# A four-stage transformer kernel on one core: routing rows turned by VectorE, norms' biases on GpSimd, and two more early products

## The chip, the cores and the metric

The kernel runs on one core of one Trainium2 chip. A core has five engines, each with its own instruction queue: TensorE (PE in the profile; its weight loads are shown apart as PEld), VectorE (DVE), ScalarE (ACT), GpSimd (POOL) and SyncE (SP), which issues most transfers. The engines wait for each other through semaphores; each takes its own instructions in order. SBUF and PSUM are memories of 128 partitions; TensorE writes its results to PSUM, from where DVE and ACT fetch them.

The metric is the time of one execution on the device, in microseconds (us). The kernel before took 1895.78 us, the median of 3 runs (1893.15 to 1896.54).

## The reference, cut to what matters

Sixteen sequences of 256 rows x 256 features go through four gated sublayers, all in 32-bit floats:

```
x = x + tanh(g_xattn[0]) * perceiver_attention(ctx, norm(x))     # stage 0: 16 heads of 64
x = x + tanh(g_ffn[0])   * experts(norm(x))                      # stage 1: 8 experts, 2 for each row
x = x + tanh(g_xattn[1]) * attention(norm(x), ctx, ctx)          # stage 2: 16 heads of 16
x = x + tanh(g_ffn[1])   * gated_linear_attention(norm(x))       # stage 3
```

`norm` is (x - mean) / sqrt(variance + 1e-5) over a row's 256 features. In stage 0 the row is normalised once by the outer norm (`y`) and once more by the attention's own (`xn`); the 77 context rows of each sequence are normalised too (`cn`). The experts' part needs the router first: `softmax(norm(x) @ router_w.T)` over 8 experts, the two largest of each row, their weights, and for each chosen expert `row @ expert_weights[e]`. The product with the router contracts over the features, so it needs the normalised rows with features on the partitions, that is turned.

## The kernel before, in words

The work is cut by sequence ("block" b, 0 to 15). A block's rows are two tiles of 128 rows, so a tile `x[b]` is 128 partitions x 2 x 256. Stage 0 takes about 960 us, and the routing of stage 1 is woven into it: while block b is in attention, block b-1 is normalised, turned and multiplied with the router, and block b-2 is ranked and scattered to the experts' lists in memory.

Stage 0 (`stage0_fast`, from line 548) runs over units (b, g), four units g = 0 to 3 a block, each with four heads. In a unit the engines get, in this order:

- `ahead_of[g]` (line 740): small work of the routing and statistics of later blocks. For g = 2: `route.weigh` of b-2 and `route.stats` of b-1.
- `scores` (line 671): products of queries and keys into three PSUM pairs `sc`, each followed by an exponential on ACT into `e`. The first pair reads the first half of `qk`, the second pair also the second half, from its second quarter on.
- `behind_scores[g]` (line 742): for g = 2 `route.norm` of b-1, which makes the normalised rows `rxn` on ACT.
- `sums` (line 689): POOL adds up `es` and `esum`.
- `values` (line 698) of the unit before: products into `o`, then on DVE a reciprocal and a product into `oT`.
- for g = 1 the turn of the next block's attention input and the projection of the block before.
- `behind_values[g]` (line 746): for g = 2 `route.ranks` of b-2 and `route.turn` of b-1, for g = 3 `route.logits` of b-1, which reads the turned rows `rxnT`.
- for g = 2 `all_values` of the next block (line 630): 16 records of products `v` (24 where a new tile of context rows comes in), with the halves copied from PSUM by ACT and then DVE.
- `heads` (line 657), twice: queries and keys of the next unit. PE writes a pair, ACT copies the queries and then DVE the keys into `qk`, which the next unit's `scores` reads.

All these calls go through `dve`, `act`, `pool` and `pe`, wrappers (`Pinned`, line 42) that keep the instructions of each engine in the order in which they are written. The order by hand is thus the order of each queue. PSUM has four pairs in stage 0, handed out in turn: a new pair waits for the readers of the pair four places before it.

`Route.turn` (line 404) turns the two row tiles of `rxn` with four PE transposes (128x128) into one PSUM pair `rtr`, from which ACT copies 128 x 512 elements to `rxnT`. It is called for blocks 0 to 14 in stage 0, and for block 15 at the start of stage 1 (line 1176).

The norms are in three steps. `moments` (line 199) has DVE compute mean and variance (`bst`, `mv`), and then a scale `rs[:, 0]` = (variance + eps)^-0.5, by POOL in two instructions or, with `by_act`, by ACT. `normed` (line 215) has DVE compute the bias `rs[:, 1]` = -mean x scale, and then ACT apply scale and bias to the 256 features of each row tile. `moments` is called for `x`, `y` and the context in stage 0 and for the routing, in stage 2's preparation (`Prepare.stats`, line 1230) and in stage 3 (`stats`, line 1631). Stage 3 has a `norm` of its own, which reads mean and scale but no bias.

Before the first unit (lines 759 to 769) the norms of block 0 go one after the other, with `warm` products in between: products of 256 columns on PE whose results nobody reads. Each fp32 product of this kind is two records in the profile.

Only `layers` with checks on (the fast version) is described here; a second copy behind a test at the end runs only if bounds are broken.

Of the kernel before, what the change touches and what calls it, by code (L numbers as in the profile page):

```python
# [10 lines left out]
F32 = mybir.dt.float32  # L11
I32 = mybir.dt.int32
AF = mybir.ActivationFunctionType
ALU = mybir.AluOpType
# [3 lines left out]
P = 128  # L18
B, S, D = 16, 256, 256
# [54 lines left out]
def layers(ctx: ExitStack, tc: tile.TileContext, t, out, check):  # L74
# [7 lines left out]
    def const(name, shape, dtype=F32):  # L82
        return cp.tile(list(shape), dtype, tag=name, name=name)
# [22 lines left out]
    ws1 = s1.enter_context(tc.tile_pool(name="s1w", bufs=1, side="right"))  # L106
# [7 lines left out]
    def c_count(j):  # L114
        return min(P, c_rows - P * j)

    def c_pieces(b):

        lo, hi = b * S2, (b + 1) * S2
        return [(j, max(lo, P * j) - P * j, max(lo, P * j) - lo, min(hi, P * j + P) - max(lo, P * j))  # L120
                for j in range(lo // P, (hi - 1) // P + 1)]

    def load_c(b):
        if b in c_new:
            j, n = c_new[b], c_count(c_new[b])
            cs[b] = ctxs.tile([P, D], F32, tag="c", name="c")
            nc.sync.dma_start(out=cs[b][:n], in_=t["ctx"].rearrange("b s d -> (b s) d")[P * j:P * j + n])
# [36 lines left out]
    ident = const("ident", [P, P])  # L164
# [10 lines left out]
    dve, act, pool, pe = (Pinned(tc, x) for x in (nc.vector, nc.scalar, nc.gpsimd, nc.tensor))  # L175
# [23 lines left out]
    def moments(src, p=P, n=2, by_act=False):  # L199
        mv = st.tile([P, 2, 2], F32, tag="mv", name="mv")  # L200
        rs = st.tile([P, 2, 2], F32, tag="rs", name="rs")
        bst = st.tile([P, 2, 6], F32, tag="bst", name="bst")
        for i in range(n):
            dve.bn_stats(bst[:p, i, :], src[:, i, :])
        for i in range(n):
            dve.bn_aggr(mv[:p, i, :], bst[:p, i, :])
        if by_act:
            act.activation(rs[:p, 0, :n], mv[:p, :n, 1], AF.Ln, bias=eps[:p])
            act.activation(rs[:p, 0, :n], rs[:p, 0, :n], AF.Exp, scale=-0.5)
            return mv, rs  # L210
        pool.tensor_scalar(rs[:p, 0, :n], mv[:p, :n, 1], 1.0, EPS, ALU.mult, ALU.add)
        pool.tensor_tensor(rs[:p, 0, :n], rs[:p, 0, :n], nhalf[:p, :n], ALU.pow)
        return mv, rs

    def normed(dst, src, mv, rs, p=P, n=2):
        dve.scalar_tensor_tensor(rs[:p, 1, :n], mv[:p, :n, 0], -1.0, rs[:p, 0, :n], ALU.mult, ALU.mult)
        for i in range(n):
            act.activation(dst[:, i, :], src[:, i, :], AF.Identity, bias=rs[:p, 1, i:i + 1],
                           scale=rs[:p, 0, i:i + 1])
# [165 lines left out]
    class Route:  # L385
# [11 lines left out]
        def stats(self, b):  # L397
            self.mv[b] = moments(xs[b])
# [3 lines left out]
            normed(self.xn[b], xs[b], *self.mv.pop(b))  # L402

        def turn(self, b, bank):
            self.xnT[b] = ws1.tile([P, 2, S], F32, tag="rxnT", name="rxnT")
            ps = bank("rtr")
            for k in range(2):
                for i in range(2):
                    pe.transpose(ps[:, (2 * k + i) * P:(2 * k + i + 1) * P], self.xn[b][:, i, k * P:(k + 1) * P], ident)
            act.copy(self.xnT[b], ps.rearrange("p (k s) -> p k s", k=2))  # L410

        def logits(self, b, bank):
            ps, xnT = bank("rt"), self.xnT.pop(b)
# [117 lines left out]
    if fast:  # L531
        route = Route()
# [15 lines left out]
    def stage0_fast():  # L548
        with ExitStack() as sx:
# [8 lines left out]
            def bank(name):  # L558
                return pair(name)[:, 0, :]
# [3 lines left out]
            xn, cn, kvT, v, oT, ctxT = {}, {}, {}, {}, {}, {}  # L563
# [5 lines left out]
            y, mvs, tallies = {}, {}, []  # L569

            def norm_c(b):
                if b in c_new:
                    n = c_count(c_new[b])
                    mvs[b, "c"] = moments(cs[b][:n].unsqueeze(1), n, 1)

            def norm_x(b):
                mvs[b, "x"] = moments(xs[b])

            def norm_y(b):
                mvs[b, "y"] = moments(y[b])  # L580

            def normed_y(b):
                y[b] = w1.tile([P, 2, D], F32, tag="y", name="y")
                normed(y[b], xs[b], *mvs.pop((b, "x")))
# [32 lines left out]
            def some_values(x, n):  # L617

                both = pair("v")
                for h in range(2):  # L620
                    for k in range(2):
                        pe.matmul(both[:n, h, :], x[:, k, :], wkv0[:, k, 1024 + h * 512:1024 + (h + 1) * 512],
                                         start=k == 0, stop=k == 1)
                return both

            def copied(to, both, n):
                act.copy(to[:n, :512], both[:n, 0, :])
                dve.tensor_copy(to[:n, 512:], both[:n, 1, :])

            def all_values(b, *between):  # L630

                v[b] = w2.tile([P, 3, 1024], F32, tag="v", name="v")
                between = list(between)
                if b in c_new:
                    j = c_new[b]
                    n = c_count(j)
                    both = some_values(ctxT[j][:, :, :n], n)
                    vc = w1.tile([P, 1024], F32, tag="vc", name="vc")
                    copied(vc, both, n)
                    if b == 0:  # L640
                        copied(v[b][:, 2, :], both, S2)
                    for to in range(1, B):
                        for jj, at, row, n in c_pieces(to):
                            if jj == j:
                                nc.sync.dma_start(out=vctx[to][row:row + n], in_=vc[at:at + n, :])
                if b > 0:
                    nc.sync.dma_start(out=v[b][:S2, 2, :], in_=vctx[b])
                for c in range(2):
                    copied(v[b][:, c, :], some_values(kvT[b][:, :, chunks[c]], P), P)
                    if between:  # L650
                        between.pop(0)()
                for x in between:
                    x()
# [72 lines left out]
            def tally():  # L726
                for rd, to in tallies:
                    act.activation(rd, rd, AF.Identity, accum_out=to)
                tallies.clear()

            def project(b):
                both = pair("proj")
                for i in range(2):
                    for m in range(8):
# [8 lines left out]
                             1: [(route.scatter, -3, 2)],  # L743
                             2: [(route.norm, -1), (route.scatter, -3, 3)],
                             3: [(normed_y, 2), (route.scatter, -2, 0)]}
            behind_values = {2: [(route.ranks, -2, bank), (route.turn, -1, bank)], 3: [(route.logits, -1, bank)]}

            def run(steps, b, g):
                for f, d, *a in steps.get(g, ()):
                    if 0 <= b + d < B:  # L750
                        f(b + d, *a)

            def warm(src, n):

                ps = bank("warm")
                for _ in range(n):
                    pe.matmul(ps[:, :D], ones, src, start=True, stop=True)
# [2 lines left out]
            warm(xs[0][:, 0, :], 3)  # L760
            normed_y(0)
            mvs[0, "y"] = moments(y[0], by_act=True)
            warm(y[0][:, 1, :], 2)
            norm_c(0)
            normed_all(0)
            turn(0)
# [5 lines left out]
            for n, (b, g) in enumerate(units):  # L772
                ahead = units[n + 1] if n + 1 < len(units) else None
                if n > 0:
                    run(ahead_of, b, g)
                now = scores(b, g)
                if g == 0 and b + 2 < B:
                    load_c(b + 2)
                if n == 0:

                    norm_c(1)
                    norm_x(1)
                    normed_y(1)
                    norm_y(1)
                else:
                    run(behind_scores, b, g)
                if n == 1:
                    normed_all(1)
                    clear_rows()
                now = sums(*now)  # L790
                if behind is not None:
                    values(*behind, by_chunk=n == 1)
                if g == 1 and b + 1 < B:
                    turn(b + 1)
                if g == 1 and b > 0:
                    project(b - 1)
                run(behind_values, b, g)
                if g == 2 and b + 1 < B:
                    all_values(b + 1, *route.weighted(b - 2))
                if ahead is not None:  # L800
                    heads(*ahead, 0)
                    heads(*ahead, 1)
                if g == 2 and b + 1 == B:
                    pieces = route.weighted(b - 2)
                    pieces[0]()
                if g == 3 and b + 1 == B:
                    pieces[1]()
                    pieces[2]()
                tally()
                behind = now  # L810
# [1339 lines left out]
```

## Time and profile before

| | |
|---|---|
| median of 3 runs | 1895.78 us |
| the profiled execution | 1900.88 us |
| its span, first to last instruction | 1899.1 us |
| mean granted TensorE clock | 0.993 |
| PE busy | 1872.1 us, 99% |
| PEld busy | 1310.1 us, 69% |
| DVE busy | 1085.0 us, 57% |
| ACT busy | 867.4 us, 46% |
| POOL busy | 986.0 us, 52% |
| stage 0 | about 11 to 960 us |
| stage 1, experts | about 960 to 1045 us alone, then with stage 2's start |
| stage 2 | to about 1220 us |
| stage 3 | to the end |

How to read it: busy time is the time in which an engine has at least one instruction running, as a share of the span. Products on PE are pipelined, so that PE at 99% isn't PE at its peak. The chain of work that ended last is followed back from the last instruction, at each step to what released it; an engine that has most of the chain is the bound. In timeline rows come start, length, engine, line, instruction, the written and the read tile, shapes, a count, and in brackets the idle time of the engine before it with what ended it. Tiles go by their names in the program with numbers left out: `rtr` is the pair of the routing's turns, `rxn` and `rxnT` are the routing's normalised rows and the turned ones, `rs` the scales and biases, `rd` the reciprocals. The line L50 is the wrapper's own line, which nearly all instructions share.

### The profile page before, as it was taken

Reading aid. Unit: us, or ns where it says so; the run is one execution under the profiler, and the core shown is the slowest. Engines: PE = TensorE matmul, PEld = TensorE weight load, DVE = VectorE, ACT = ScalarE, POOL = GpSimd, SP = SyncE. Lnnn points to the kernel's source line nnn. Section 1 sums busy time; section 2 is a strip of 40 time slices with the busy share of each in tenths; the row PEclk is TensorE's granted clock in tenths of the full one; section 3 lists DMA queues with packets and bytes.
Section 4 is the critical chain, followed back from the end, with each engine's and each line's share of the span. In section 5 each row is a group of like instructions: output and inputs, shape, how many; then the busy total and the mean of one; then the engine's idle time right before and its main releaser. Section 6 shows DMA issues by size and latency. Waiting matters only on the chain.

```text
span 1899.1 us, 34899 instructions
## 1 busy us (share of the span) xinstructions
PE 1872.1 (99%) x13916; PEld 1310.1 (69%) x13916; DVE 1085.0 (57%) x2632; ACT 867.4 (46%) x1804; POOL 986.0 (52%) x879
## 2 busy tenths in 40 slices
PE   8999999999999999999999999999999999999997
PEld 5666676666766666666787666667777777777775
DVE  3334545445645546543573488876666666666664
ACT  4333344444444344343333488744445444454443
POOL 4653757556675567655725756124444444444433
PEclk9999999999999999999999899999999999999999
DMA  9500000100010000000178723000000000000000
GB/s 323 191 4 19 23 26 15 33 11 21 22 36 11 27 16 12 28 30 12 35 254 252 176 44 50 7 1 6 7 7 7 6 12 7 7 7 7 12 6 14
DMA packets 56901, 84.63 MB, mean 45 GB/s; under 512 B 10467, under 2 KB 44371, under 8 KB 56217
## 3 DMA queue, kind: packets, MB, share of 16 engines
q1 hardware_dynamic: 44441, 65.52, 10.4%
q0 software_dynamic: 12288, 16.79, 4.3%
q8 instruction: 112, 1.84, 0.4%
q14 instruction: 60, 0.49, 0.1%
HBM read 44.00 MB, written 38.29 MB: 43 GB/s over the span
## 4 chain that ended last, share of the span: by engine, by line
PE 95%; DVE 2%; ACT 1%; DMA 0%; issue 0%; POOL 0%; SPq 0%; DVEq 0%; POOLq 0%; ACTq 0%
PE o L50 14%; PE qk L50 13%; PE sc L50 11%; PE v L50 8%; PE proj L50 7%; PE kq L1607 6%; PE sc L1607 5%; PE gq L1607 3%; PE ex L50 3%; PE v L1607 3%; PE proj L1607 3%; PE o L1607 3%; PE gz L1607 2%; PE den L1607 2%; PE low L1607 1%; PE ms L1607 1%
## 5 line engine op out<-in xcount | busy, mean ns | idle before, releaser
L50 POOL TENSOR_SCALAR rs<-mv 128x2 f32<-128x2 f32 (+2 forms) x85 | 16.3, 192 | 443.7 <-DVE mv L50 440.6
L50 ACT ACTIVATE e<-sc 128x1024 f32<-128x1024 f32 (+1 forms) x192 | 181.6, 1016 | 18.1 <-PE sc L50 18.1
L50 PE MATMUL sc<-qk 64*128 64x256 f32 (+1 forms) x1536 | 183.1, 384 | 0.5 <-DVE qk L50 0.5
L50 DVE RECIPROCAL rd<-o 128x256 f32<-128x256 f32 x64 | 112.4, 1756 | 116.2 <-PE o L50 116.2
L50 PE MATMUL o<-e,v 128*32 128x256 f32 (+1 forms) x3072 | 177.9, 379 | 0.0
L50 PEld LDWEIGHTS sc<-qk 64*128 64x128 f32 (+1 forms) x1536 | 132.0, 172 | 55.4 <-issue 27.6
L50 POOL TENSOR_TENSOR esum<-esum,es 128x512 f32<-128x512 f32 x128 | 162.4, 1269 | 10.0
L50 POOL TENSOR_TENSOR es<-e 128x1024 f32<-128x1024 f32 x64 | 151.2, 2362 | 27.0 <-ACT e L50 24.3
L50 PE MATMUL qk<-kvT,wkv 128*128 128x333 f32 x512 | 164.3, 443 | 0.0
L50 ACT ACTIVATE qk<-qk 128x256 f32<-128x256 f32 x128 | 49.0, 383 | 235.9 <-PE qk L50 235.9
L50 POOL TENSOR_TENSOR es<-es,e 77x1024 f32<-77x1024 f32 x64 | 150.1, 2346 | 5.0
L50 POOL TENSOR_TENSOR k<-e,ee 128x256 f32<-128x256 f32 x64 | 46.7, 730 | 192.0 <-ACT e L50 192.0
L50 PEld LDWEIGHTS o<-e,v 128*32 128x32 f32 (+1 forms) x3072 | 99.8, 110 | 66.3
L50 DVE COPY qk<-qk 128x333 f32<-128x333 f32 x128 | 64.7, 505 | 125.9 <-ACT qk L50 124.4
L50 PE MATMUL qk<-kvT,wq 128*128 128x256 f32 x512 | 134.2, 384 | 0.0
L50 POOL TENSOR_TENSOR at<-at,at 128x768 f32<-128x768 f32 x63 | 113.9, 1808 | 24.7 <-DVE at L50 23.9
L50 DVE TENSOR_TENSOR at<-sc,amask 128x768 f32<-128x768 f32 x64 | 61.3, 958 | 113.7 <-PE sc L1607 110.1
L50 POOL DMA_INDIRECT x<-rows_out,pos x64 | 100.1, 1564 | 34.7 <-issue 15.6
L50 PEld LDWEIGHTS qk<-kvT,wkv 128*128 128x128 f32 x512 | 97.2, 190 | 30.0
L50 PEld LDWEIGHTS qk<-kvT,wq 128*128 128x128 f32 x512 | 94.3, 189 | 33.8 <-issue 11.7
L50 PE MATMUL proj<-wo0h,oT 128*128 128x256 f32 x512 | 113.5, 380 | 0.0
L50 PE MATMUL v<-wkv,kvT 128*128 128x512 f32 x256 | 112.5, 592 | 0.0
(253 smaller groups left out, 4093.1 us busy)
## 6 DMA issues: line engine op xcount, KB each, us to landing
rows<-zero SPq DMA_DIRECT2D x16, 640.0 KB
xin<-rows SPq DMA_DIRECT2D x16, 640.0 KB
rows_out<-y SPq DMA_DIRECT2D x16, 384.0 KB
v<-vctx SPq DMA_DIRECT2D x15, 308.0 KB
x<-in_x_dram SPq DMA_DIRECT2D x16, 256.0 KB
rows_out<-y SPq DMA_DIRECT2D x16, 256.0 KB
out_dram<-x SPq DMA_DIRECT2D x15, 256.0 KB
wkv<-in_wkv_dram SPq DMA_DIRECT2D x2, 1024.0 KB
```

What stands on the lines that cost most here:

```text
L50: x = getattr(self.engine, name)(*a, **k)
L1607: tc.keep_in_program_order(nc.tensor.matmul(*a, **k))
```

## The change

Three edits, none of which alters what is computed.

- `Route.turn` called without a PSUM bank turns the rows on DVE, in squares of 32: for each group q of 32 rows and each group r of 32 features (within a half of 128) one `dve.transpose` that takes four squares, over the two row tiles and the two feature halves. That is 16 instructions a block, SBUF to SBUF, without PE, PSUM or ACT. Blocks 0 to 14 are turned so, at g = 2 behind `all_values` and ahead of `heads`; block 15 keeps the way of before.
- The bias leaves `normed`. `moments` computes it right behind the scale: by POOL in two instructions, or by DVE where ACT made the scale (`by_act`). Stage 3, which calls `moments` too, gets the two POOL instructions as well.
- Before the first unit, `warm` on `y` makes 4 products where it made 2.

```diff
@@ moments
             act.activation(rs[:p, 0, :n], rs[:p, 0, :n], AF.Exp, scale=-0.5)
+            dve.scalar_tensor_tensor(rs[:p, 1, :n], mv[:p, :n, 0], -1.0, rs[:p, 0, :n], ALU.mult, ALU.mult)
             return mv, rs
         pool.tensor_scalar(rs[:p, 0, :n], mv[:p, :n, 1], 1.0, EPS, ALU.mult, ALU.add)
         pool.tensor_tensor(rs[:p, 0, :n], rs[:p, 0, :n], nhalf[:p, :n], ALU.pow)
+
+        pool.tensor_tensor(rs[:p, 1, :n], mv[:p, :n, 0], rs[:p, 0, :n], ALU.mult)
+        pool.tensor_scalar(rs[:p, 1, :n], rs[:p, 1, :n], -1.0, None, ALU.mult)
         return mv, rs
@@ normed
-        dve.scalar_tensor_tensor(rs[:p, 1, :n], mv[:p, :n, 0], -1.0, rs[:p, 0, :n], ALU.mult, ALU.mult)
@@ Route.turn
         def turn(self, b, bank):
-            self.xnT[b] = ws1.tile([P, 2, S], F32, tag="rxnT", name="rxnT")
+            xnT, xn = ws1.tile([P, 2, S], F32, tag="rxnT", name="rxnT"), self.xn[b]
+            self.xnT[b] = xnT
+            if bank is None:
+
+                for q in range(0, P, 32):
+                    for r in range(0, P, 32):
+                        dve.transpose(xnT[r:r + 32].rearrange("p k (i s) -> p i k s", i=2)[:, :, :, q:q + 32],
+                                      xn[q:q + 32].rearrange("p i (k d) -> p i k d", k=2)[:, :, :, r:r + 32])
+                return
             ps = bank("rtr")
...
@@ stage0_fast
-            behind_values = {2: [(route.ranks, -2, bank), (route.turn, -1, bank)], 3: [(route.logits, -1, bank)]}
+            behind_values = {2: [(route.ranks, -2, bank)], 3: [(route.logits, -1, bank)]}
...
-            warm(y[0][:, 1, :], 2)
+            warm(y[0][:, 1, :], 4)
...
                 if g == 2 and b + 1 < B:
                     all_values(b + 1, *route.weighted(b - 2))
+                if g == 2 and b > 0:
+                    route.turn(b - 1, None)
                 if ahead is not None:
                     heads(*ahead, 0)
                     heads(*ahead, 1)
```

## The prediction

> **What bounds the kernel now.** I read the chain that ended last first. It is PE's nearly throughout:
>
> ```profile
> PE 95%; DVE 2%; ACT 1%; DMA 0%; issue 0%; POOL 0%; SPq 0%; DVEq 0%; POOLq 0%; ACTq 0%
> ```
>
> So a microsecond taken from PE's stream is won, and one in which PE waits is lost, whatever the other engines' shares are. Next comes the timeline of stage 0 around a unit with g = 2, the place of the edit (start, length, engine, instruction, idle time before it). PE's own answer:
>
> ```profile
> 289.08 0.63 PE L50 MATMUL rtr<-ident,rxn 128*128 128x128 f32 x4
> 289.55 7.03 PE L50 MATMUL v<-wkv,kvT 128*128 128x512 f32 x16
> 296.42 1.03 PE L50 MATMUL qk<-kvT,wq 128*128 128x256 f32 x4
> ```
>
> and the one with all engines, further on:
>
> ```profile
> 297.24 0.69 DVE L50 COPY v<-v 128x512 f32<-128x512 f32 x1 [2.74 <-ACT v L50]
> ...
> 299.11 0.51 DVE L50 COPY qk<-qk 128x333 f32<-128x333 f32 x1 [1.18 <-ACT qk L50]
> ...
> 300.48 2.86 PE L50 MATMUL sc<-qk 64*128 64x256 f32 x24
> ```
>
> The reader is to see two things. The four turns hold PE from 289.08 to 289.55, so 0.47 us a block. And after the second v copy DVE has one job on which PE depends: the qk copy, over at 299.62, which the scores of g = 3 read at 300.48. From the end of the v copy (297.93) to the scores there are 2.55 us, of which the copy needs 0.51. I looked at eleven blocks; the distance is 2.55 to 2.56 in each.
>
> Third, the granted clock. One block, b = 2, shows what a short wait of PE costs here (stretches of 1 us: PE's busy time, then the clock):
>
> ```profile
> 166.00:167.00 1.00, 0.07 (x1) 1.00 0.00 0
> 167.00:168.00 1.00, 0.72 (x4) 0.96 0.00 0
> 168.00:169.00 1.00, 1.00 (x4) 0.50 0.00 0
> 169.00:170.00 1.00, 1.00 (x3) 0.50 0.00 0
> 170.00:171.00 1.00, 1.00 (x2) 0.50 0.00 0
> 171.00:172.00 1.00, 1.00 (x3) 0.83 0.00 0
> ```
>
> PE idles 1.21 us (0.93 + 0.28); then the clock is at half for 3.4 us, and the chain's stretch of 24 v records takes 11.90 us where other blocks with 24 take 10.30. So 1.2 us of waiting cost 1.6 us more. The wait's cause stands in the timeline:
>
> ```profile
> 164.05 2.37 POOL L50 TENSOR_TENSOR es<-e 128x1024 f32<-128x1024 f32 x1
> 164.12 2.31 DVE L50 SCALAR_TENSOR_TENSOR rs<-mv,rs 128x2 f32<-128x2 f32 x1 [1.10 <-POOL rs L50]
> ```
>
> A bias of two elements, 0.16 us elsewhere, ended only with the GpSimd operation beside it; the row's normalisation and PE's turn waited for it.
>
> **The change, part by part.**
>
> *Turns off PE.* 15 blocks (b = 0 to 14; the last keeps PE) x 0.47 = 7.1 us from the path; the chain gives the turns 0.8% of 900 us, 7.2. ACT loses 15 copies of 0.586 us, off the path: nothing. With the turns, b = 2's wait on the normalised rows goes: 1.2 + 1.6 = 2.8 us.
>
> *Turns on DVE.* Each block adds 16 instructions of 32 partitions x 128 elements, SBUF to SBUF, between the second v copy and the two qk copies, in DVE's written order. No such instruction is in the trace. Below: small operations that don't need each other start 0.08 to 0.12 us apart (283.60, 283.67, 283.80, 283.88), so 16 x 0.10 = 1.6 us. Above: the nearest form, 32 partitions x 128 elements, from PSUM with a scalar per partition:
>
> ```profile
> L50 DVE TENSOR_SCALAR low<-low,vec 32x128 f32<-32x128 f32 x30 | 10.5, 350 | 0.7
> ```
>
> Two of these follow one 128x256 of 0.475 us and go to another group of 32 partitions each; the three together take 1.22 us, that is 0.475 + 2 x 0.35 and 0.02 between. They run end to end, where two bn_stats on all partitions (0.41 each, 0.74 together) overlap by 0.07. For an SBUF source I take DVE's sums (128x16 in 0.167, 128x512 in 0.692): 0.15 us + 1.04 ns an element, 0.283 for 128. The new turns change the partition group with each instruction, as the 32x128 rows do, so I add the 0.02 and round up for filling a square: 0.31 us each, 5.0 a block. Overlapped they would take 0.22 (3.5); with two passes over the data 0.15 + 0.27 = 0.42 (6.7). I take 5.0, since the 32x128 row is the nearest.
>
> The first turn can start 0.07 before the v copy's end, at 297.86; 16 end at 302.86; the qk copy at 303.37; PE sees it 0.05 later. The scores start at 303.42, not 300.48: **PE waits 2.95 us**. In general the wait is the turns' time less 2.05. Nothing absorbs it: heads are done, the scores are next in PE's order. The second qk copy is 0.5 us behind the first and needed 1.4 us into the scores. The last block has no values in front; there the oT product ends at 933.03, and the wait is 933.03 + 5.0 + 0.5 - 935.41 = 3.1 us, or 3.6 against a PE that is 0.47 earlier: taken as the others.
>
> [...]
>
> *The clock behind the wait.* At the price of b = 2, each wait of 2.95 us brings 3.4 us at half clock: 1.7 us. Bounds: nothing (between 8 and 12 us PE idles 2.0 of 4 us in two pieces and the clock stays 1.00), and 10.2 us at half clock, 5.1 us (from 1079.3, after 1.6 us of idling in small pieces). I take 1.7, the row with one wait in stage 0.
>
> [...]
>
> *Biases on GpSimd.* 69 of the 74 biases leave DVE, and 85 pairs (stage 3's unused ones too) go to POOL behind the power: a product at 0.20 (rsum 128x4, 202 ns), a scaling at 0.19, and 0.09 before each: 0.57 us. Queued behind are the scatters and the es sums; es of a unit is done at 296.03 and read at 303.27, which covers 0.57. y, rxn and xn on ACT come 0.3 to 0.4 us later; y, at 306.6, is read at 312.45, and PE no longer waits for rxn. Without that cover each would cost up to 0.4 us a block. The rows of stage 3 don't read the bias. Nothing, but for b = 2 above.
>
> *Start.* The first y's bias now stands ahead of the ctx statistics in DVE's order and waits for ACT until 8.20; these start at 8.31, not 7.55 (0.76), and the ctx bias takes POOL 0.57 where DVE took 0.29. So cn starts at 10.46, not 9.43: 1.0 us, on the path, since PE waits for cn. The two warm products are four records 0.21 apart, 0.86 us, into the 0.82 that PE idles there (8.36 to 9.18): nothing; if the clock fell there without them, a gain up to 1.6.
>
> **Sum**, on the profiled execution: 15 x (2.95 + 1.7 - 0.47) = 62.7; less 2.8, plus 1.0: +61. The profiled execution took 1900.9 us (span 1899.1), 5.1 above the median of the runs, so 1962 on its scale and **1957** on the median's.
>
> **Rivals.**
> 1. *The clock doesn't fall* (for: the idling before 12 us): 15 x 2.48 - 1.8 = +35, 1931.
> 2. *Faster: the turns fit into the slack.* The place is the 2.05 us between v copy and qk copy; the decisive point is the wait that the savings pay, (7.1 + 1.8) / 15 = 0.6 us, a turn of 2.65 / 16 = 0.165 us. Under 0.128 all is hidden: 1895.8 - 8.9 = 1887. For: 0.10 between small independent operations. Against: 128 elements at the 1.04 ns of DVE's rows are 0.133 without any start.
> 3. *The turns overlap* (0.22): a wait of 1.45; without a drop 15 x 0.98 - 1.8 = +13, 1909; with one +38, 1934.
> 4. *The clock stays down for 10.2 us*: 15 x 7.58 - 1.8 = +112, 2008. For: scores and o use part of the array, as stage 2's products did. Against: b = 2 recovered in 3.4.
> 5. *The change doesn't do what it says*, the queue order being other than written: within 9 us of before.
>
> **How the numbers follow.** Forecast 0.48 (1940 to 1982, the upper end from 0.42 a turn); rival 1 0.18; rival 2 0.10; rival 3 0.12; rival 4 0.09; rival 5 0.03. The range 1905 to 1998 leaves out rivals 2, 4 and 5 (0.22), of rival 4 only what stays down in most blocks. A measurement of this kernel tells 0.2% (3.8 us) from no change: faster 0.11, same 0.04, slower 0.85.
>
> **What would show it.** DVE's group of transposes: 240, mean near 0.31 us, 5.0 a block. The scores' idle time before them: 15 times about 3 us, released by the DVE qk copy. The clock: under 1.00 in each block of stage 0 behind g = 2. cn near 10.5 us. No rtr on PE but the last block's four. If turns average under 0.165 us, or the qk copies aren't behind them, the forecast is wrong in sign; if the waits are there and the clock stays at 1.00, it is rival 1.

## The result, and the profile after

The changed kernel takes 1950.2 us, the median of 4 runs (1947.92 to 1952.27), against 1895.63 us for the kernel before in the same comparison (1893.15 to 1896.54). The ratio is 1.0279, with a 95% interval of 1.0260 to 1.0298: 54.6 us slower, where the prediction said 61. The profiled execution took 1949.22 us, its span 1947.4.

The chain that ended last, page of the changed kernel:

```profile
PE 89%; DVE 7%; ACT 2%; issue 1%; DMA 0%; POOL 0%; SPq 0%; POOLq 0%; ACTq 0%
```

DVE had 2% of it before. A chain names who was late, not what it cost: it now runs through whole rows of turns (15 x 5.03 us, 4% of the span by its line for `rxnT`), while PE waited about 3 us a block for them. What was lost stands in the timeline around g = 2, in the rows of PE (start, length, engine, instruction, idle time before it with what ended it):

```profile
298.14 7.11 PE L50 MATMUL v<-wkv,kvT 128*128 128x512 f32 x16
305.09 1.03 PE L50 MATMUL qk<-kvT,wq 128*128 128x256 f32 x4
...
307.94 1.28 PE L50 MATMUL qk<-kvT,wkv 128*128 128x333 f32 x4
312.14 4.55 PE L50 MATMUL sc<-qk 64*128 64x256 f32 x24 [2.92 <-DVE qk L50]
```

and in those of DVE, same stretch:

```profile
305.90 0.69 DVE L50 COPY v<-v 128x512 f32<-128x512 f32 x1 [2.74 <-ACT v L50]
306.51 5.03 DVE L50 STREAM_TRANSPOSE rxnT<-rxn 32x128 f32<-32x128 f32 x16
311.58 0.92 DVE L50 COPY qk<-qk 128x333 f32<-128x333 f32 x2
```

No `rtr` stands ahead of the v products any more. The turns start when the second v copy is nearly done, and the qk copy that the scores read comes behind all 16 of them. PE has finished the heads and stands still for 2.92 us. And the scores, 2.86 us before, then take 4.55. The granted clock says why (stretches of 1 us: PE's busy time, then the clock):

```profile
311.00:312.00 1.00, 0.00 (x0) 1.00 0.00 0
312.00:313.00 1.00, 0.86 (x8) 0.94 0.00 0
313.00:314.00 1.00, 1.00 (x8) 0.50 0.00 0
314.00:315.00 1.00, 1.00 (x6) 0.50 0.00 0
315.00:316.00 1.00, 1.00 (x8) 0.50 0.00 0
316.00:317.00 1.00, 1.00 (x14) 0.86 0.00 0
```

That is 3.41 us at half clock, 1.71 us lost. One block earlier, behind a wait of the same length, it isn't so:

```profile
252.00:253.00 1.00, 0.00 (x0) 1.00 0.00 0
253.00:254.00 1.00, 0.85 (x8) 1.00 0.00 0
254.00:255.00 1.00, 1.00 (x14) 1.00 0.00 0
255.00:256.00 1.00, 1.00 (x14) 1.00 0.00 0
```

The table of PE's waits in stage 0 (total, times, longest) and the tile `rxnT` (count, shortest/median/longest in ns) give the totals; the 16th wait, of 0.46 us, is another one:

```profile
PE sc L50 <- DVE qk L50: 44.8, 16, 3.5
```

```profile
L50 DVE STREAM_TRANSPOSE rxnT<-rxn x240: 289/302/308, 118.9 to 986.9; 32x128 f32<-32x128 f32 x120
```

Fourteen waits are of 2.92 us, the last block's is 3.48: 44.4 us. Ten of the fifteen bring a drop of the clock: 17.1 us. At b = 2, where the kernel before had its one long wait, nothing is left of it: PE is busy from 163 to 173 us at clock 1.00. The first `xT`, with which stage 1 begins, comes at 1007.6 us, not 953.5: stage 0 alone lost 54.1 us. The rest of the profiled execution got 5.8 us shorter, mainly since that of before had lost 5.1 us of clock at the entry of stage 2 and this one loses none there.

POOL's busy time went from 986.0 to 1024.9 us, with the biases among its groups between 60 and 1000 us (busy, mean ns, idle before):

```profile
L50 POOL TENSOR_TENSOR rs<-mv,rs 128x2 f32<-128x2 f32 x43 | 8.5, 197 | 3.4
L50 POOL TENSOR_SCALAR rs<-rs 128x2 f32<-128x2 f32 x43 | 9.5, 222 | 3.8
```

### The profile page after: what moved, and what is told of

It is laid out like the page before. It is cut to its first block, busy times and chain, and to the rows that moved or that the text cites. A ratio compares the mean times of both kernels' runs of the same rounds, so it can differ in the third digit from the quotient of the medians.

```text
span 1947.4 us, 35176 instructions
## 1 busy us (share of the span) xinstructions
PE 1878.5 (96%) x13860; PEld 1312.3 (67%) x13860; DVE 1119.0 (57%) x2803; ACT 859.4 (44%) x1789; POOL 1024.9 (53%) x1049
## 4 chain that ended last, share of the span: by engine, by line
PE 89%; DVE 7%; ACT 2%; issue 1%; DMA 0%; POOL 0%; SPq 0%; POOLq 0%; ACTq 0%
PE o L50 13%; PE sc L50 11%; PE qk L50 10%; PE v L50 8%; PE proj L50 7%; PE kq L1620 6%; PE sc L1620 5%; DVE rxnT L50 4%; PE gq L1620 3%; PE ex L50 3%; PE v L1620 3%; PE proj L1620 3%; PE o L1620 3%; PE gz L1620 2%; PE den L1620 1%; PE low L1620 1%
## 5 line engine op out<-in xcount | busy, mean ns | idle before, releaser
L50 PE MATMUL sc<-qk 64*128 64x256 f32 (+1 forms) x1536 | 199.0, 409 | 44.8 <-DVE qk L50 44.8
L50 PEld LDWEIGHTS sc<-qk 64*128 64x128 f32 (+1 forms) x1536 | 141.1, 183 | 105.6 <-DVE qk L50 55.2
```

The costliest lines, as they stand in the source:

```text
L50: x = getattr(self.engine, name)(*a, **k)
```

## The experiments

The theory is that of the prediction: 16 turns end to end on DVE hold the qk copy, PE waits 2.92 us, and the clock answers some of the waits. It was tried by parting the change, by stretching and filling the wait, by moving the turns, and by measuring the turn itself. Diffs are against the changed kernel unless said otherwise.

**Only biases and warm products.** The turn goes back to PE:

```diff
-            behind_values = {2: [(route.ranks, -2, bank)], 3: ...
+            behind_values = {2: [(route.ranks, -2, bank), (route.turn, -1, bank)], 3: ...
-                if g == 2 and b > 0:
-                    route.turn(b - 1, None)
```

> The changed kernel with the turns given back to PE; the biases on GpSimd and the four warm products stay. Theory A (the loss is the 16 turns in DVE's order ahead of the qk copies, plus the clock that falls behind the wait): the 2.9 us waits of the scores are gone, the time is that of before, 1894 us (1888 to 1900): plus 1.1 at the start, less 2.9 in block 2 where the bias no longer blocks. Rival B (the biases' 170 GpSimd instructions or the start cost it): above 1920 us.

Measured: 1898.38 us (11 runs), ratio 1.0004 (0.9995 to 1.0013). The waits of the scores are gone, and stage 0 ends at 951.6, 1.9 us before the kernel before's 953.5: 2.9 gained at b = 2, 1.3 lost at the start (first v product at 12.94, not 11.68). Its profiled execution then lost 8.5 us of clock near 1080 us, at stage 2's entry. In the median the two edits cost nothing that can be measured; the 1.6 us that this sum promises don't show there either.

**Only the turns.** The kernel before with the turns on DVE; biases and warm products as they were:

```diff
@@ moments
-            dve.scalar_tensor_tensor(rs[:p, 1, :n], ...
...
-        pool.tensor_tensor(rs[:p, 1, :n], ...
-        pool.tensor_scalar(rs[:p, 1, :n], ...
@@ normed
+        dve.scalar_tensor_tensor(rs[:p, 1, :n], mv[:p, :n, 0], -1.0, rs[:p, 0, :n], ...
...
-            warm(y[0][:, 1, :], 4)
+            warm(y[0][:, 1, :], 2)
```

> The kernel before with only the turns on DVE; biases and warm products as before. Theory A: 15 waits of the scores of 2.9 us and about 10 clock drops, 1949 us (1943 to 1955). Rival B: near 1900 us.

Measured: 1949.78 us, 1.0282 (1.0263 to 1.0301); 15 waits, 44.4 us, and eleven drops of the clock where about ten were expected. The loss is the turns'.

**Twice as many turns.** Each is issued twice in a row, on the same squares; the second writes what the first wrote:

```diff
-                    for r in range(0, P, 32):
+                    for r in (r for r in range(0, P, 32) for _ in range(2)):
```

> Each of the 16 turns is issued twice in succession with the same squares; the result is unchanged. Theory A: the wait grows by what the second 16 cost. If an instruction is held only when its partition group changes, the repeat costs 0.22 us, not 0.31: turns 8.5 us a block, waits 6.4 us, about 2005 us; if every turn waits for the one before, 10.0 us a block, waits 7.9 us, about 2028 us. If the turns weren't on the path: 1950 us.

Measured: 2043.32 us, 1.0770 (1.0754 to 1.0787). Timeline of that kernel, one block:

```profile
325.06 10.43 DVE L50 STREAM_TRANSPOSE rxnT<-rxn 32x128 f32<-32x128 f32 x32
...
336.09 5.49 PE L50 MATMUL sc<-qk 64*128 64x256 f32 x24 [8.32 <-DVE qk L50]
```

32 turns last 10.43 us where 16 last 5.03, and the wait is 5.40 longer: PE pays each added microsecond of turns in full. The clock now falls at all fifteen waits, for 6.8 or 10.2 us; about half of that lies within the waits themselves, so that 30.9 us are lost by it in stage 0 (half of PE's busy time in the drops). The 15 waits come to 125.3 us where 15 x 7.9 were expected, and waits and clock together put the time above the expected 2028. This run leaves open whether two turns could overlap, as both of a pair write the same place.

**The wait filled.** Six products that nobody reads, behind the heads:

```diff
+                if g == 2 and b > 0:
+                    warm(wq0[:, 0, :D], 6)
```

> The changed kernel with six unread products of 256 columns on PE (2.6 us) between the heads of g = 2 and the scores that wait. Theory A: they lie in the wait of 2.92 us, PE idles 0.4 us instead and the clock stays at 1.00: 10 drops of 1.7 us fewer, 1933 us (1928 to 1938). Rival C (the drops aren't caused by the wait): 1950 us. If PE were the bound there, not the wait: 1988 us.

Measured: 1937.13 us, 1.0209 (1.0194 to 1.0225). PE's rows in one block:

```profile
305.56 2.75 PE L50 MATMUL warm<-wq,ones 128*128 128x256 f32 x12
...
308.64 2.86 PE L50 MATMUL sc<-qk 64*128 64x256 f32 x24 [0.33 <-DVE qk L50]
```

The scores take 2.86 us again, and stage 0 loses no clock: the drops are the idle PE's, not another effect of the turns. Stage 0 ends 16.8 us before the changed kernel's (990.8, not 1007.6), close to the 17.1 of the drops. The median is 13.1 us lower; this kernel's profiled execution lost 3.4 us of clock at the entry of stage 2, the changed kernel's none. What stays, 40 us over the kernel before, is the wait itself, now filled with useless work.

**The turns in DVE's own gaps.** DVE waits 2.74 us for nearly every v copy (timeline above), 1.6 to 1.7 for the first one in some blocks. Eight turns are put ahead of the first v copy and eight between the two; the last block, which has no v copies, keeps PE:

```diff
-                    all_values(b + 1, *route.weighted(b - 2))
-                if g == 2 and b > 0:
-                    route.turn(b - 1, None)
+                    if b > 0:
+                        turns = (lambda: route.turn(b - 1, None, 0, 8)), (lambda: route.turn(b - 1, None, 8, 16))
+                    all_values(b + 1, *route.weighted(b - 2), turns=turns)
```

> The changed kernel with the 16 turns split: 8 ahead of the v copies and 8 between the first and the second v copy, where DVE idled 2.6 and 2.7 us before; the last block of the 15 keeps PE. Theory A: 8 turns take 2.5 us, the scores wait for nothing, and the savings stand alone: 14 x 0.47 and block 2's 2.9, plus 1.1 at the start: 1887 us (1882 to 1892). Rival D (turns slow down or stop beside GpSimd's sums, which run in just these gaps, as the bias of block 2 did): turns of well over 0.31 us, waits remain, 1900 us or more.

Measured: 1887.16 us (6 runs, 1885.55 to 1890.47), 0.9945 (0.9930 to 0.9960). **This version is faster than both kernels,** if only by 0.55% than the one before. Timeline, all engines:

```profile
288.11 2.50 DVE L50 STREAM_TRANSPOSE rxnT<-rxn 32x128 f32<-32x128 f32 x8
288.51 2.35 POOL L50 TENSOR_TENSOR es<-es,e 77x1024 f32<-77x1024 f32 x1
290.62 0.69 DVE L50 COPY v<-v 128x512 f32<-128x512 f32 x1
291.33 2.52 DVE L50 STREAM_TRANSPOSE rxnT<-rxn 32x128 f32<-32x128 f32 x8
293.88 0.69 DVE L50 COPY v<-v 128x512 f32<-128x512 f32 x1
295.67 0.51 DVE L50 COPY qk<-qk 128x333 f32<-128x333 f32 x1 [1.10 <-ACT qk L50]
297.05 2.86 PE L50 MATMUL sc<-qk 64*128 64x256 f32 x24
```

The same turns with the same lengths cost PE nothing here: the qk copy is over at 296.18, 0.87 us before the scores need it. POOL's sum beside the first eight doesn't slow them (303 ns in the median, 302 in the changed kernel). Stage 0 ends at 946.1.

**The same, with the context's norm first at the start:**

```diff
+            norm_c(0)
             mvs[0, "y"] = moments(y[0], by_act=True)
             warm(y[0][:, 1, :], 4)
...
-            norm_c(0)
```

> As the kernel with the turns in the gaps, and the first context tile's statistics ahead of the first y's on DVE. Theory A: the context's chain is off the start's path, 1.1 us less: 1886 us. Rival: y's statistics come later by the 0.6 us of the context's and the start gains nothing, 1887 us.

Measured: 1888.61 us (6 runs), 0.9956 (0.9940 to 0.9972). The first v product starts at 12.14, not 12.83 us; the two versions' times can't be told apart.

**Four turns early, twelve at the change's place:**

```diff
+                        turns = (lambda: route.turn(b - 1, None, 0, 4)), (lambda: route.turn(b - 1, None, 4, 4))
...
-                    route.turn(b - 1, None)
+                    route.turn(b - 1, None, 4 if b + 1 < B else 0, 16)
```

> The changed kernel with 4 of the 16 turns ahead of the v copies and 12 where the change has them. Theory A: 12 turns take 3.77 us, so the scores wait 1.66 us. In the changed kernel the clock fell exactly where one of the consecutive stretches of 3.413 us held 2.02 us or more of the wait, and not where it held 1.72 or less; so no block drops: 1914 us (1908 to 1920). Rival E (any wait above 1.2 us drops the clock, as in block 2 of before): 10 to 15 drops, 1931 to 1940 us.

Measured: 1921.07 us, 1.0120 (1.0099 to 1.0141). PE's waits from 60 to 1110 us:

```profile
PE sc L50 <- DVE qk L50: 28.2, 15, 3.5
```

Fourteen waits are of 1.76 us (0.10 over the expected 1.66), and none brings a drop. The last block kept its 16 turns, which the expectation overlooked: a wait of 3.48 us and the only drop of stage 0 behind the start. Small extras (1.7 us of clock at 13 us, 3.4 at stage 2) make the time just over the expected range.

**All turns behind both heads,** that is behind the qk copies:

```diff
-                if g == 2 and b > 0:
-                    route.turn(b - 1, None)
                 if ahead is not None:
                     heads(*ahead, 0)
                     heads(*ahead, 1)
+                if g == 2 and b > 0:
+                    route.turn(b - 1, None)
```

> The changed kernel with all 16 turns behind both heads' copies instead of ahead of them. Theory A: the wait moves on instead of going: DVE is 5 us late into g = 3, its reciprocal comes 2.7 us late and the qk copy for the next unit 2 us late, of which 1.1 us show as a wait of the next scores; no clock drop: 1904 us (1895 to 1915). Rival: DVE's idle time in g = 3 takes the turns in: 1887 us.

Measured: 1948.45 us, 1.0266 (1.0244 to 1.0288): neither number. The waits of PE, 60 to 1110 us, and the timeline of one block:

```profile
PE o L50 <- POOL es L50: 32.4, 20, 3.6
PE sc L50 <- DVE qk L50: 10.9, 12, 0.9
```

```profile
308.40 5.04 DVE L50 STREAM_TRANSPOSE rxnT<-rxn 32x128 f32<-32x128 f32 x16
...
315.96 0.19 POOL L50 TENSOR_SCALAR rs<-mv 128x2 f32<-128x2 f32 x1 [12.01 <-DVE mv L50]
...
319.59 2.86 PE L50 MATMUL sc<-qk 64*128 64x256 f32 x24 [0.90 <-DVE qk L50]
...
325.46 1.08 PE L50 MATMUL o<-es,ones 128*32 128x256 f32 x8 [3.01 <-POOL es L50]
```

The wait moved on. The turns now hold the statistics (`mv`) of the next rows. POOL comes to their scale in its order and stands there for 12 us; the `es` sums are written behind it, and PE's o products wait for these. POOL had stood there for 7.88 us in the kernel before. With 9.4 us lost by the clock that is 52.7 us, against 61.5 (44.4 + 17.1) in the changed kernel; stage 0 ends at 1003.0, 4.6 us earlier, and the medians are hardly apart. What was 5 us late on DVE was still 3 us late on PE, through two engines. The prediction's sentence that es has 7 us of cover was true for 0.57 us of added POOL work, not for a POOL held by DVE.

**The turn by itself.** A block's turns in 32 halves of 64 elements, in two orders. First, the two halves with the same partition groups in succession; then the group changes with each instruction:

```diff
+                for q, r, i in [(q, r, i) for q in range(0, P, 32) for r in range(0, P, 32) for i in range(2)]:
+                    dve.transpose(xnT[r:r + 32, :, i * P + q:i * P + q + 32], ...
```

```diff
+                for i, q, r in [(i, q, r) for i in range(2) for q in range(0, P, 32) for r in range(0, P, 32)]:
```

> Each of the 16 turns cut in two of 64 elements (one row tile each), the two of a pair in succession: they read and write the same groups of 32 partitions, in different places. By the sum for a turn, 0.15 us + 1.04 ns an element + 0.03, one of 64 elements takes 0.25 us. Theory F (a turn waits for the one before only when the partition group changes): the second of a pair starts 0.07 us earlier, 32 take 6.8 us, waits of the scores 4.7 us. Theory G (every turn waits for the one before): 7.9 us, waits 5.8 us.

> The same 32 half turns, all of one row tile before those of the other, so that the group written changes with each. Theories F and G both: 7.9 us a block, waits 5.8 us. Beside the paired order this is the control: only under F is the paired one shorter, by 1.1 us a block.

Measured, one run each beside 1897.73 us for the kernel before: 1972.38 and 2021.27 us. Rows of DVE, the first kernel, then the second:

```profile
311.26 6.00 DVE L50 STREAM_TRANSPOSE rxnT<-rxn 32x64 f32<-32x64 f32 x32
```

```profile
318.93 7.96 DVE L50 STREAM_TRANSPOSE rxnT<-rxn 32x64 f32<-32x64 f32 x32
```

The same 32 instructions on the same data take 6.00 or 7.96 us by their order alone, and the scores' 15 waits 58.9 or 88.3 us in all. 16 of the steps keep the group in the first order: 1.96 / 16 = 0.12 us saved at each, where 0.07 had been expected (6.8 us a block). In the change every step alters the group, and its turns start 0.315 us apart at a length of 0.302: nothing overlaps. What holds a turn whose group differs from that of the one before isn't shown; the two runs give what the difference costs.

**Two warm products.** The version with the context first, and 2 products on `y` in place of 4:

```diff
-            warm(y[0][:, 1, :], 4)
+            warm(y[0][:, 1, :], 2)
```

> The kernel with the turns in the gaps and the context's statistics first, with 2 warm products on y in place of 4. If the 4 products end later than the normalised rows and so set the start there (in its trace the first attention turn stood at 10.37 us and cn had ended at 9.98), the first v product of block 0 comes 0.5 to 0.9 us earlier than 12.14 us; if the clock needs them, the products after 12 us run at half speed and the start is later.

Measured, one run: 1892.42 us, with the first v product at 12.20 us; 12.14 with four. The heads come at 24.95 instead of 22.55 us. The first four v records with two warm products, then the first five with four:

```profile
12.20 3.78 PE L50 MATMUL v<-wkv,ctxT 128*128 128x512 f32 x4 [0.96 <-DVE ctxT L50]
```

```profile
12.14 2.41 PE L50 MATMUL v<-wkv,ctxT 128*128 128x512 f32 x5 [0.96 <-DVE ctxT L50]
```

The records start 0.85 us apart until 16.6 us where they start 0.43 apart with four: half speed. The profile's clock column reads 1.00 there, but only because it has no record yet: the trace's first one, at full clock, starts at 16.95 us; in the changed kernel, with four, at 9.09. So the two added products can be worth 2.4 us. The kernel with the turns alone, also with two, shows the same (first record at 16.64, heads at 24.78). The kernel before, with two, had its first record at 7.50 and its heads at 22.08, so that they aren't always needed.

## Why the prediction was right, and where it wasn't

Stage 0's share, by the prediction's own terms (profiled executions, us):

| term | predicted | measured |
|---|---|---|
| 15 waits of the scores | 44.3 | 44.4 |
| clock behind them | 25.5 | 17.1 |
| turns off PE | -7.1 | not measured apart; -7.1 taken |
| b = 2 | -2.8 | -2.9 |
| start | +1.0 | +1.2 |
| sum | +61 | +52.7; stage 0 lost 54.1 |

- **A turn's length.** 0.31 us and 5.0 a block were predicted, 0.302 and 5.03 measured; 0.315 from start to start. The sum of rows gave 0.303; the rounding up "for filling a square" had no row behind it, and no run shows such a cost. The row it was taken from (32x128 from PSUM, 0.350 us) gave the right view, that nothing overlaps, and the two orders of halves showed that a step that alters the group costs 0.12 us more than one that keeps it. Rivals 2 and 3 needed turns of 0.165 and 0.22. (The small operations of the lower bound start 0.07 to 0.13 us apart, not 0.08 to 0.12; the forecast doesn't rest on it.)
- **The wait** is the turns' time less a slack of 2.05 us: 2.92 against 2.95 in the change, 1.76 with twelve turns late. The last block's is 3.48 (3.1 to 3.6 predicted). With twice the turns it grew by what these grew, and with the turns in DVE's gaps it was gone. The place decided, not the instruction.
- **The clock is the term that was mis-sized.** "Each wait of 2.95 us brings 3.4 us at half clock": the price was right, 3.41 us and 1.71 lost, but ten waits of fifteen paid it, 17.1 us where 25.5 were put. A single block (b = 2) was taken for the rule, and how many waits pay changes with the execution: eleven with the turns alone. How near the forecast came is thus in part luck of phase. Rival 1, no drop at all, and rival 4, 10.2 us each, were both wrong in this stage. The idling before 12 us that spoke for rival 1 is in four pieces, not two, and lies in two stretches of the clock's beat (last section), 1.27 and 0.76 us.
- **Turns and b = 2.** Only taken out with the waits do they show: the version with the turns in the gaps ends stage 0 at 946.1, 7.4 us before the kernel before, expected 7.1 x 14/15 + 2.9 - 1.2 = 8.3.
- **Biases on GpSimd** cost nothing, as said (ratio 1.0004 together with the warm products). Their cover held where POOL itself wasn't held; where DVE held POOL for 12.01 us (turns behind both heads), PE's o products waited 3.01 us.
- **The start** lost 1.16 us (v product at 12.84, not 11.68), as worked out (1.0). The warm products gained nothing visible against the profiled execution before, whose clock was full from 7.50 us; where two products weren't enough (above), they are worth more than the 1.6 us that the prediction set as their bound.
- **The scale.** The prediction took the profiled execution's surplus of 5.1 us over the median into account; it is as much as the clock lost at stage 2's entry in that execution (5.12 us), which the executions lose or not: between 0 and 8.5 us in the profiles of this study.

## What to carry to other kernels

An engine that has nearly half its time free (DVE was busy for 57% of the span) can still hold the kernel up with 5.03 us in the wrong place of its queue (2.92 us of waiting a block): look for what stands behind the new work in that queue, and put the work where the engine waits anyway, not where it is written most easily. When it is moved, ask the same question again at the new place, through every engine that waits in order. And a wait on PE is to be priced with the clock that it costs behind it (1.71 us behind ten of these fifteen), which here depended on chance of timing as much as on its length.

## What the runs showed of the hardware

- **The clock's drops keep a beat.** In the changed kernel the ten drops of stage 0 start at 125.14, 190.00, 312.88 and so on to 988.71 us: all whole multiples of 3.4133 us apart (863.57 = 253 x 3.4133), though the blocks aren't. If time is cut into stretches at that beat and each wait is divided over them, the clock fell where one stretch held 2.02 us of waiting or more (ten waits) and stayed where the larger part was 1.72 or less (five). With the turns alone the smallest that dropped was 1.96 and the largest that didn't 1.77; with twelve turns late none of the fourteen waits of 1.76 dropped; behind the heads the two were 2.09 and 1.92. So a wait of under about 1.9 us was free of it there, one of 2.92 a matter of phase, and one of 8.32 always hit. This is inferred from the places of the drops. It isn't the whole rule: the kernel before's drop at b = 2 (167.93 us, 267 beats before its next at 1079.29) came behind a stretch that held only 1.21 us of idling, among o, rank and rtr products. What counts beside the idle time stays open.
- **At the start, look at the records, not at the clock column.** With two warm products the first clock record came at 7.50 us in one kernel and at 16.64 and 16.95 in two others; until then the column prints 1.00, while in the last of these the v records are 0.85 us apart instead of 0.43. In the changed kernel, with four, it came at 9.09.
- **Two engines beside each other**: one of the 74 biases, a DVE operation with two inputs, ended 2.31 us after its start beside a POOL sum in the kernel before (median 0.16); turns, with one input, kept their 303 ns beside the sums. Whether the number of inputs is the reason wasn't tried.
